# A two-layer perceiver on one core: another table of due times for the kernel's own planner

## The chip, the cores and the metric

The kernel runs on one core of one Trainium2 chip. The core has five engines with a queue of instructions each: PE (TensorE, matmuls and transposes, which write to PSUM), DVE (VectorE), ACT (ScalarE), POOL (GpSimd) and SP (SyncE, which here issues all DMA transfers). Each engine takes its own instructions strictly in the order in which the program has them, and waits on semaphores for what the others make. The metric is the time of one execution on the device in microseconds (us).

## The reference

128 sequences of 32 latent rows of 256 numbers (`x`) read a context of 257 rows each (`ctx_1024`). All is float32. Six steps, each added to `x`, each on a layer norm of `x`:

```python
x = x + _L0_xattn_ref(ctx_1024, ln(x), wq, wk, wv)   # softmax attention of x over the context
x = x + _L0_attn_ref(ln(x), W_in, W_gate, W_out, ...) # a selective scan along the 32 rows
x = x + _L0_ffn_ref(ln(x), W_fc, ln_w, ln_b, W_proj)  # gelu MLP with ternary weights
x = x + _L1_xattn_ref(ln(x), ctx, ctx, Wq, bq, ...)   # linear attention, focused feature map
x = x + _L1_attn_ref(ln(x), W_q, W_k, W_v, W_o, ...)  # attention over 32 rows, decaying scores
x = x + _L1_ffn_ref(ln(x), w1, b1, w2, b2)            # MLP with 8-bit activations, ternary weights
```

The scan is the recurrence `h = h * exp(A * d_t) + (x_t * d_t) * B`, `y_t = h @ c0`, over 512 channels with 16 states each.

## The kernel before

**Tiling.** Four sequences make a group of 128 rows, one tile of 128 partitions; there are 32 groups. The groups are taken in nine blocks, `BLOCKS = (2, 4, 4, 4, 4, 4, 4, 4, 2)`. In each block:

- `context_group` for each group: loads `x`, the context `cx` and its last row `cr`; transposes them on PE (`pT`, `pcT`); computes the query product `pq`, the scores `psc`, the softmax on ACT and DVE, `po`, `py`, and adds to `x`. A second part makes the keys and values that step four needs later: `pkey` (PE), `ku` (relu on ACT, then two products on POOL), `ks` (squares with sums on ACT), `kn` and `kf` (powers on POOL), `pval` (PE), `vf` (ACT) and `pk` (PE), whose result is `kvc`.
- `scan_block` for the whole block: gates and projections (`pproj` on PE), then, for each of four slices of channels and 16 states, `a` (exponential on ACT), `h` (the scan on DVE) and a weighted sum, `acc` on DVE or `h` and `some` on POOL. The last two blocks give six of the 16 states to POOL instead of two. It ends with `yg` on DVE and `pout` on PE.
- `latent_group` for each group: `mlp`, `linear`, `attention`, `quantized_mlp`, each a chain of short steps from engine to engine, and the store of the result.

Before the first block stands the setup of weights: among others the chain of small `sp_y` and `sp_z` operations on DVE, which leads to `isp`, `bkp`, `bk`, on PE `pisp`, `pbk`, `pkl`; loads of `w_in`, `w_gate`, `wv0` (in the profile `wv`) and others stand in SP's queue at the start.

**The planner.** The kernel doesn't issue its operations as the Python code meets them. A `Recorder` collects them all, with what each needs and an assumed duration (`ns_of`), and `Recorder.order` sorts them before anything is issued. A group of matmuls inside `R.together()` is one operation. `begin` and `part` cut the record into 251 spans: each `context_group` has two, each `scan_block` six, each `latent_group` four, the setup the rest. For each span the table `DUE` has a pair, the due time of its first operation and the end; operations between get due times in proportion to the assumed durations. One unit is about one block of the work. `AHEAD` is subtracted for transfers:

```python
a, b = self.spans[op.group]
due.append(a + (b - a) * (d - op.ns) / total[op.group] - AHEAD * ("sync" in op.ways))
```

The planner then places one operation after another. On each engine it looks at those that are ready, takes of those that could start within `WINDOW` ns of the earliest the one that is due first (`SOONER` favours those that free PSUM), and among the engines the one that would start first. `HORIZON` limits how far ahead of the oldest open work a buffer may be opened. An operation that two engines can do (a copy, a relu, the casts `x<-xT`) goes where its start plus its duration, weighed with `PRICE`, is least. The order of placing is the order in which all engines' queues are filled; a dependency without a semaphore keeps each engine's order. All of this runs when the program is built; on the chip only the resulting order is left.

**Lines in the profile.** Every recorded operation is issued by one line of `trace`, so nearly every row has the line L575 and is told apart by its tiles. L562 is `keep_busy`: where the plan leaves PE idle for more than `GAP` = 600 ns ahead of the first write to a bank of PSUM, it puts filler matmuls into that bank, `int(FILL * (op.gap - 200.0) / 216.0)` of them, with no result that anybody reads.

## Time and profile before

| | |
|---|---|
| three runs | 1745.08, 1747.30, 1744.87 us; median 1745.08 |
| the profiled execution | 1747.35 us, its span 1745.6 us |
| mean granted PE clock in it | 0.987 |
| matmuls of L562 | 172 |
| table loads on ACT | 95 shown, 121.9 us |
| DMA | 59.74 MB, mean 34 GB/s; 222 GB/s in the first 45 us |
| last `h` scan of the last block, end of its `yg` | 1633.1 us |
| last `yg` of the block before | 1509.3 us |

The costliest groups of instructions are the scans `h` on DVE (576 of them, 613.3 us), the exponentials `a` on ACT (576, 366.8 us), the sums `acc` on DVE (436, 299.5 us), and on PE `pval` and `pkey` (1024 each, 245.5 and 238.1 us). In a group's row the columns are engine and operation, out<-in by tile names, shapes, count, busy us and mean ns of one, and the idle time of that engine just before with what ended it. A mark in time such as "the last `yg` of a block" was found by putting the trace's instructions of each engine beside the recorded operations in order.

### The profile page before, as it was taken

The page shows a single profiled execution, that of the slowest core. Times are in us where ns is not written, and L with a number is a line of the kernel's source. Part 1 is how long each engine was busy: PE and PEld are TensorE (multiplying, and loading weights), DVE is VectorE, ACT ScalarE, POOL GpSimd, SP SyncE. Part 2 cuts the span into 40 slices and gives each one's busy share as a digit, 9 for nine tenths or more (in the row PEclk, how much of TensorE's full clock was granted, in tenths as well). Part 3 has the DMA queues.
Part 4 walks back from the last instruction along what each step waited for, and adds up shares of the span by engine and source line. Part 5 has one row for each costly group of instructions (what it writes and reads, how often), then busy time and mean ns, then how long its engine had stood idle before and what let it go on. Part 6 is the DMA issues. An engine that isn't in the chain of part 4 may idle for free.

```text
span 1745.6 us, 45752 instructions
## 1 busy us (share of the span) xinstructions
PE 1657.3 (95%) x17523; PEld 1203.7 (69%) x17591; DVE 1508.2 (86%) x2956; ACT 1426.8 (82%) x3495; POOL 1356.6 (78%) x2145
## 2 busy tenths in 40 slices
PE   8999999999999999999999999999999988888996
PEld 5777777776776777767777677776777665656663
DVE  5479689989988999988999799979999899988866
ACT  3677698889987999879887989888888898777665
POOL 4766758678776988778788779867888799878887
PEclk9999999999999999999999999999999999999998
DMA  7312000111000011001110021001110000000000
GB/s 221 107 45 86 29 29 29 45 41 32 10 29 29 8 64 38 29 2 41 35 35 29 8 62 41 29 2 35 41 35 29 4 23 1 7 1 2 8 8 19
DMA packets 44762, 59.74 MB, mean 34 GB/s; under 512 B 8704, under 2 KB 27008, under 8 KB 44544
## 3 DMA queue, kind: packets, MB, share of 16 engines
q1 hardware_dynamic: 44544, 56.81, 10.1%
q8 instruction: 139, 2.28, 0.6%
q14 instruction: 79, 0.65, 0.1%
HBM read 52.32 MB, written 4.19 MB: 32 GB/s over the span
## 4 chain that ended last, share of the span: by engine, by line
PE 39%; DVE 28%; ACT 14%; POOL 13%; issue 4%; DMA 0%; DVEq 0%; POOLq 0%; ACTq 0%
DVE h L575 13%; PE pval L575 6%; DVE acc L575 6%; PE pkey L575 6%; PE pproj L575 4%; ACT a L575 3%; PE pT L575 3%; POOL ku L575 2%; POOL rstd L575 2%; ACT ks L575 2%; PE pqa L575 2%; PE pmlp L575 2%; ACT L575 2%; PE pk L575 2%; DVE st L575 2%
## 5 line engine op out<-in xcount | busy, mean ns | idle before, releaser
L575 DVE TENSOR_TENSOR_SCAN h<-a,pproj 128x512 f32<-128x512 f32 (+1 forms) x576 | 613.3, 1086 | 22.4 <-ACT a L575 17.6
L575 ACT ACTIVATE a<-dl,a_neg 128x496 f32<-128x496 f32 (+1 forms) x576 | 366.8, 664 | 71.3 <-DVE h L575 68.4
L575 DVE SCALAR_TENSOR_TENSOR acc<-h,w_st,acc 128x512 f32<-128x512 f32 (+1 forms) x436 | 299.5, 687 | 0.6
L575 PE MATMUL pval<-wkv,cT 128*128 128x256 f32 x1024 | 245.5, 386 | 1.4 <-DVE y L575 1.3
L575 PE MATMUL pkey<-wkv,cT 128*128 128x256 f32 x1024 | 238.1, 386 | 0.0
L575 ACT ACTIVATE ks<-ku 128x256 f32<-128x256 f32 x512 | 209.0, 415 | 16.8 <-POOL ku L575 15.5
L575 PEld LDWEIGHTS pkey<-wkv,cT 128*128 128x128 f32 x1024 | 189.3, 190 | 38.0 <-issue 14.9
L575 PEld LDWEIGHTS pval<-wkv,cT 128*128 128x128 f32 x1024 | 188.9, 191 | 31.4 <-issue 2.8
L575 POOL TENSOR_TENSOR ku<-ku,e 128x512 f32<-128x512 f32 x128 | 162.7, 1281 | 33.9 <-ACT ku L575 28.3
L575 POOL TENSOR_TENSOR ku<-ks,ku 128x512 f32<-128x512 f32 x128 | 165.4, 1300 | 18.7 <-ACT ks L575 17.8
L575 POOL TENSOR_TENSOR kn<-kn,halves 128x4 f32<-128x4 f32 x128 | 131.1, 1026 | 24.4 <-ACT ks L575 23.4
L575 POOL TENSOR_TENSOR rstd<-rstd,halves 128x1 f32<-128x1 f32 x224 | 125.8, 565 | 7.3
L575 ACT ACTIVATE vf<-pval,kf 128x256 f32<-128x256 f32 x256 | 107.4, 472 | 23.2 <-PE pval L575 15.5
L575 ACT ACT_TABLE_LOAD x95 | 121.9, 1283 | 1.7
L575 PE MATMUL pproj<-xTs,w_in 128*128 128x512 f32 (+1 forms) x288 | 122.4, 552 | 0.3
L575 POOL TENSOR_SCALAR rstd<-mv 128x1 f32<-128x1 f32 x224 | 45.2, 202 | 96.6 <-DVE mv L575 73.2
L575 POOL TENSOR_TENSOR some<-some,h 128x512 f32<-128x512 f32 (+1 forms) x104 | 115.1, 1107 | 2.8
L575 PE MATMUL pmlp<-w_pr,hT 128*128 128x256 f32 x512 | 116.7, 381 | 0.0
L575 PEld LDWEIGHTS pmlp<-w_pr,hT 128*128 128x128 f32 x512 | 95.6, 190 | 13.8 <-issue 0.8
L575 ACT ACTIVATION_READ_ACCUMULATOR ks<-ku 128x1 f32 x512 | 100.6, 196 | 0.0
L575 POOL TENSOR_SCALAR h<-h,w_st 128x512 f32<-128x512 f32 (+1 forms) x104 | 65.3, 630 | 40.7 <-DVE h L575 35.5
L575 PE MATMUL ph<-w_fc,x 128*128 128x512 bf16 x350 | 89.2, 379 | 5.3 <-ACT ku L575 1.4
(291 smaller groups left out, 3883.7 us busy)
## 6 DMA issues: line engine op xcount, KB each, us to landing
cx<-in_ctx_dram SPq DMA_DIRECT2D x64, 512.0 KB
x<-in_x_dram SPq DMA_DIRECT2D x32, 128.0 KB
cr<-in_ctx_dram SPq DMA_DIRECT2D x128, 32.0 KB
out_dram<-x SPq DMA_DIRECT2D x32, 128.0 KB
vlz<-vl SPq DMA_DIRECT2D x128, 1.1 KB
w_in<-in_w_inT_dram SPq DMA_DIRECT2D x1, 1024.0 KB
raw_fc<-in_w_fcT_dram SPq DMA_DIRECT2D x2, 512.0 KB
raw_pr<-in_w_prT_dram SPq DMA_DIRECT2D x2, 512.0 KB
```

Source lines behind the costliest of these rows:

```text
L575: ins = getattr(engine, name)(*(traced(a) for a in args), **{k: traced(v) for k, v in kw.items()}).ins
```

## The change

Only numbers change: the five constants of the planner other than `GAP` and `FILL`, and nearly all of the 251 pairs of `DUE`. The operations that are recorded, their needs, their assumed durations and the code that places them are the same.

```diff
-PRICE = {"tensor": 0.0, "vector": 20.786091, "scalar": 1.959533, "gpsimd": 3.101899, "sync": 0.0}
-WINDOW = 13.816
-SOONER = 0.066
-AHEAD = 0.777235
-HORIZON = 1.581593
+PRICE = {"tensor": 0.0, "vector": 28.013093, "scalar": 4.356996, "gpsimd": 3.720234, "sync": 0.0}
+WINDOW = 13.821085
+SOONER = 0.0675
+AHEAD = 0.744939
+HORIZON = 1.665209
...
 DUE = (
-    (-1.0, -0.7651), (0.1, 0.598373), (-1.116179, -1.019716), (-0.267211, 0.164717),
-    (0.144, 0.184841), (0.213655, 0.218655), (0.394, 0.426463), (0.439863, 0.48282),
...
-    (8.366433, 8.49925), (8.732164, 8.864981), (8.847172, 8.866054), (8.489793, 8.799099),
-    (8.733373, 8.957995), (9.049952, 9.177105), (8.969544, 9.442262), (8.255137, 8.578091),
-    (8.559023, 8.723782), (8.443238, 8.947841), (8.98058, 9.391686),
+    (-1.233024, -0.335498), (0.019828, 0.480193), (-1.629912, -0.869437), (-0.837897, -0.738361),
+    (-0.093681, -0.088914), (-0.021839, -0.017211), (0.306149, 0.488484), (0.39917, 0.543159),
...
+    (8.253436, 8.258436), (8.822697, 8.893896), (7.808234, 8.023224), (7.738237, 8.019826),
+    (7.982233, 8.675198), (8.325431, 8.442062), (7.934126, 8.201542), (8.599655, 8.919463),
+    (8.003761, 8.776671), (8.022448, 8.742972), (9.092878, 9.902772),
 )
```

The fifth and sixth pairs are those of the first context group; the last eight those of the last two latent groups. A pair need not follow the one before it, and an operation is never due before those that it needs.

## The prediction

> **What bounds the kernel now.** I read the page's shares of busy time first, then the busy time by stretch, then the chain of waits, then the timeline of the first 30 us.

> ```profile
> span 1745.6 us, 45752 instructions
> PE 1657.3 (95%) x17523; PEld 1203.7 (69%) x17591; DVE 1508.2 (86%) x2956; ACT 1426.8 (82%) x3495; POOL 1356.6 (78%) x2145
> ...
> PE 39%; DVE 28%; ACT 14%; POOL 13%; issue 4%; DMA 0%; DVEq 0%; POOLq 0%; ACTq 0%
> ```

> PE looks full, but part of its busy time is filler (L562, matmuls that keep_busy puts where the plan sees PE idle). Counted on its own, with overlaps taken once, filler is 42 us, so PE does 1615 us of the program's matmuls, and 1745.6 - 1615.5 = 130 us hold none. The windows (columns: length, busy us of PE, PEld, DVE, ACT, POOL with counts, granted clock, DMA share, GB/s) tell where they are:

> ```profile
> 0.00:60.00 60.00, 54.28 (x279) 38.05 (x280) 28.39 (x82) 23.98 (x80) 33.27 (x68) 0.94 0.65 198
> 60.00:1360.00 1300.00, 1273.83 (x13700) 935.95 (x13749) 1153.28 (x2150) 1113.56 (x2801) 1007.49 (x1569) 1.00 0.11 34
> 1360.00:1509.30 149.30, 131.84 (x1181) 91.95 (x1188) 142.30 (x230) 126.43 (x268) 127.31 (x183) 1.00 0.03 9
> 1509.30:1633.10 123.80, 106.87 (x1152) 74.38 (x1156) 106.03 (x273) 89.90 (x208) 99.42 (x172) 0.94 0.01 4
> 1633.10:1745.60 112.50, 90.51 (x1216) 63.42 (x1221) 78.25 (x224) 72.89 (x140) 89.14 (x157) 0.92 0.04 12
> ```

> From 60 to 1360 us PE is 98% busy: it sets the pace, and an order can't gain there. To 1509.3 us (the end of the scans of the last block of four groups) DVE is at 95%. To 1633.1 us (the end of the very last scan) no engine is over 86%. Behind it, 112.5 us of short dependent steps with POOL highest at 79%. An order can gain in the last two stretches and in the first 60 us, nowhere else.

> **The change part by part.** No instruction is new. Counted in the two instruction streams: PE fillers 172 to 159, casts `x<-xT` on ACT 50 to 39 and on POOL 14 to 25, table loads 96 and 96, all else equal. So what is to be costed is the order. I weighed each step by the time the trace gave its kind and summed, engine by engine, what stands ahead of a mark.

> *Start.* The loads of x and cx of the first group now stand ahead of wv0, w_in and w_gate (1.8 MB), and on PE the first group's transposes, query product and scores (`pT`, `pq`, `pcT`, `psc`) stand ahead of `pbk` and `pkl`. Before, fillers stand there and PE waits:

> ```profile
> 11.79 2.32 PE L562 MATMUL pisp<-onesb,identb 128*128 128x512 bf16 x10
> 13.95 1.46 PE L562 MATMUL pbk<-onesb,identb 128*128 128x512 bf16 x6
> 16.16 0.71 PE L575 MATMUL pisp<-diag,ones 128*128 128x128 f32 x4 [0.76 <-DVE diag L575]
> ...
> 19.16 0.99 PE L575 MATMUL pbk<-ident,bkp 128*128 128x128 f32 x4 [2.07 <-DVE bkp L575]
> 20.67 0.37 PE L575 MATMUL pkl<-bk,onesb 3*128 3x256 bf16 x1 [0.52 <-DVE bk L575]
> ```

> Before, the first `pkey` starts at 27.85, after `pT`, `pq` and `pcT` from 22.83 to 26.89. With these done earlier and a `pT` of 0.4 us in their place it can start near 23.5: 4.35 us sooner. But behind it the new stream has 33 fillers where the old has 15 (58 and 57 in all at the start), since the next steps wait for POOL and ACT (`ku`, `ks`, `kn`), which follow `pkey` at their old speed: 18 holes more, which at 0.25 us, a `pisp` filler's own time (2.7 us for 11), take 4.5 us back. On DVE `st` and `mv` of the first x (0.42 and 0.18) now stand inside the sp_y chain, and `nmx` ahead of `bk`: should x land late, `diag`, `bkp` and so `pkl` are late by as much. Bounds -4.35 and 0.6 (the two operations); I take 0, since the holes only move.

> *60 to 1509.3 us.* Ahead of the mark stand 0.1 us more of PE, 1.4 more of DVE, 4.6 less of ACT, 7.2 more of POOL; seven lone fillers are gone, the 40 near its end stay 40. A filler's worth lies between those 0.25 us and all 130 us over 172, 0.76 us. So -1.8 to -5.3; I take -2, near the lower end, since the middle has few holes. What hides the 7.2 us of POOL is its share, 85% in the last 149 us; without that cover it costs 7.2 / 0.85 = 8.5 us.

> *To the last scan.* The stretch loses 7.0 us of DVE, 5.5 of PE, 4.6 of ACT, 9.6 of POOL, and its fillers go from 56 to 40. At the density it has now (106.2 us of DVE in 123.8, 86%) 7.0 us less is 8.2 us less. Bounds: -5.5 (PE's share alone) and -8.2 - 16 x 0.76 = -20 (the fillers' holes gone too). I take -8.

> *Behind the last scan.* What left the stretch is here: PE 81.1 to 86.4, DVE 73.7 to 79.3, ACT 70.8 to 76.6, POOL 90.1 to 96.5, fillers 12 to 21. Were the stretch to keep its density it would grow by 112.5 x 6.4 / 90.1 = 8.0 us; were the steps to fit into the idle 20% of POOL, by nothing. POOL and PE follow each other in the chain here, so I take +5.

> *Casts.* 0.405 us each on ACT, 0.397 on POOL: 11 moved are 4.4 us of work from one to the other, already in the sums. POOL can also hold DVE up:

> ```profile
> 1581.74 2.06 POOL L575 TENSOR_TENSOR kvx<-kvc,band 128x1088 f32<-128x1088 f32 x1
> 1582.02 2.06 DVE L575 TENSOR_TENSOR y<-y,zf 128x256 f32<-128x256 f32 x1
> ```

> That `y<-y,zf` takes 0.41 us elsewhere; here it ends with POOL's `kvx`. Eleven casts could cost DVE 0 to 4.4 us in this way; I take 0, as a cast is short and most sit where PE sets the pace. [...]

> The fillers also keep the clock up. Where PE waited at 17 to 19 us, the granted clock over 20 to 26 us was 0.50, and `pkl` took 674 ns a matmul against 386 for `pval`. [...]

> *Sum.* 0 - 2 - 8 + 5 + 0 = -5 us. A second way: 13 fillers fewer at 0.25 to 0.76 us are -3.3 to -9.9, and PE's own work is the same. The profiled execution took 1747.35 us (1.75 outside the span); with -5 that is 1742.35. The median of the runs is 1745.08, 2.27 below that execution, so the forecast for the median is 1740.

> **The rivals.**
> - *The end keeps its length.* The work that moved behind the last scan fits into gaps (PE has 22 us idle there, ACT 40). Then 0 - 2 - 8 + 0, and with 3 of the 4.35 us at the start -13: 1732. For it: no engine is over 79% there. Against: the last two groups run one step behind another from 1634 to 1743.
> - *All is given back.* The end grows by its full 8.0: -2, or 1743. For it: PE's work is the same, and every part that left one stretch stands in the next.
> - *GpSimd becomes the bound.* It has 7.2 us more ahead of 1509.3 and 6.4 more behind the last scan. At 85% and 80% that is +8.5 and +8.0, less 8.2 between: +8.3, or 1753, slower. It decides once POOL is over some 92% busy from 1360 to 1509 us. For it: the waits of DVE's `xn` for `rstd` and of PE for POOL's `q`, 12 us each. Against: its spare time there is 22 us.
> - *The plan isn't followed.* The order within an engine is fixed, but on the chip it waits for what is really late there, and the holes that the plan closed may open elsewhere: 1745, counted with "all is given back".

> **How the numbers follow.** Forecast (1740, itself 1735 to 1744) 0.36; end keeps its length (1732) 0.24; all given back or not followed (1743 to 1745) 0.17; GpSimd the bound (1753) 0.23. The range goes from 1727 (the -20 bound with +5, and a little of the start) to 1751, which leaves out the worst part of the last case and the best of the second. A measurement of this kernel tells 0.2%, 3.5 us. Faster than that is 1741.6 or less: all of the second case and nine tenths of the forecast's, 0.57; within, 0.20; slower, 0.23.

> **What would show it.** The last scan's end (1633.1 before) should come near 1623, and from there to the end should be 115 to 119 us; 112 or less speaks for the first rival, over 120 for the second. First `pkey` near 23.5 us, the start of the first pproj near its old 92 us. POOL from 1360 to 1509 under 90%. PE's filler rows 159. The forecast is wrong if the middle, 60 to 1360 us, moves by more than 3 us: I found nothing in it to move.

## The result and the profile after

The kernel after takes 1720.63 us (median of four runs, 1719.12 to 1721.22), the kernel before in the same session 1744.97 us (four runs, 1743.05 to 1747.30). The ratio is 0.9859, with a 95% interval of 0.9842 to 0.9876: faster by 24.3 us, where the prediction had 5, and below the low end of its range. The profiled execution of the kernel after took 1721.22 us, its span 1719.4.

First the lines of the page that answer to those shown of before (span, busy time by engine, chain of waits by engine):

```profile
span 1719.4 us, 45778 instructions
PE 1653.8 (96%) x17578; PEld 1203.7 (70%) x17578; DVE 1497.6 (87%) x2956; ACT 1422.8 (83%) x3484; POOL 1365.9 (79%) x2156
...
PE 50%; DVE 23%; ACT 14%; POOL 9%; issue 3%; DVEq 0%; POOLq 0%; ACTq 0%
```

PE's share of the chain that ended last rose from 39 to 50%, DVE's fell from 28 to 23 and POOL's from 13 to 9. Then the windows of the kernel after, cut at the same marks of the work (1493.3 us is the last `yg` of the last block of four groups, 1598.8 that of the last block, which ends the very last scan; the 1633.1 us of before is the same mark); columns as before:

```profile
0.00:60.00 60.00, 54.86 (x294) 39.09 (x295) 30.79 (x86) 25.27 (x83) 37.09 (x74) 1.00 0.65 198
60.00:200.00 140.00, 139.91 (x1567) 109.50 (x1567) 113.48 (x236) 109.14 (x336) 107.07 (x156) 1.00 0.22 67
200.00:1344.00 1144.00, 1130.10 (x12195) 824.35 (x12194) 1033.03 (x1914) 999.58 (x2451) 907.91 (x1422) 1.00 0.10 31
1344.00:1493.30 149.30, 133.50 (x1163) 92.25 (x1162) 141.07 (x230) 126.25 (x270) 128.09 (x186) 0.99 0.03 9
1493.30:1598.80 105.50, 96.17 (x943) 67.98 (x942) 97.18 (x249) 84.34 (x192) 90.23 (x154) 0.97 0.01 4
1598.80:1719.40 120.60, 99.31 (x1425) 70.57 (x1422) 82.05 (x243) 78.25 (x156) 95.51 (x169) 0.93 0.04 12
```

In the prediction's windows 60 to 1360 us of the kernel before was one row, with a clock of 1.00. Cut at 200 us it says more:

```profile
60.00:200.00 140.00, 135.30 (x1501) 106.54 (x1500) 112.12 (x233) 105.31 (x325) 91.00 (x138) 0.98 0.21 67
200.00:1360.00 1160.00, 1138.52 (x12201) 829.41 (x12250) 1041.16 (x1918) 1008.24 (x2477) 916.49 (x1432) 1.00 0.10 30
```

In the same 140 us the kernel before runs 1501 matmuls at a clock of 0.98 with 4.7 us idle, the kernel after 1567 at 1.00 with 0.1 us idle. The large differences are there and in the stretch before the last scan, which went from 123.8 to 105.5 us; the one behind it grew from 112.5 to 120.6.

The timeline of PE at the start of the kernel after, for the lines shown of before (start, length, engine, line, operation, tiles; in brackets the idle time before it and what ended it):

```profile
16.85 0.68 PE L575 MATMUL pisp<-diag,ones 128*128 128x128 f32 x4 [1.24 <-DVE diag L575]
17.37 0.60 PE L575 MATMUL pcT<-ident,cx 128*128 128x128 f32 x4
17.80 0.81 PE L562 MATMUL psc<-onesb,identb 128*128 128x512 bf16 x3
18.54 1.15 PE L575 MATMUL psc<-cT,qT 128*32 128x257 f32 x16
19.76 0.68 PE L575 MATMUL pbk<-ident,bkp 128*128 128x128 f32 x4
...
22.43 0.39 PE L575 MATMUL pkey<-bk,onesb 3*128 3x512 bf16 x2
```

`pbk` no longer waits 2.07 us; `pcT` and `psc` of the first group fill that place, and `pkey` starts at 22.43 (before: 27.85).

A ledger of PE's time shows where the 26.2 us of span went. Each interval of PE's rows is counted once, as the program's matmuls, fillers or idle; "lost by the clock" is an estimate, half the time of the program's matmuls that started while the granted clock was half (in before four `pkl` take 2.07 us at 20.97, where the clock is 0.50, and four `pval` of the same shape 1.03 us at 136.16, where it is 1.00). Where a filler overlaps the program's next matmul, the time goes to the one that started first, so that fillers come to 46.3 us here and to the prediction's 42 where they are counted only while they run alone.

| stretch (before; after) | length | idle | fillers | lost by the clock |
|---|---|---|---|---|
| to the end of the first block's scans (197.7; 188.2) | -9.5 | 10.4 to 5.1 | 14.8 to 14.9 | 6.2 to 0 |
| to the end of the sixth four-group block's scans (1355.6; 1339.4) | -6.7 | 21.4 to 14.0 | 1.9 to 0 | 0 to 0 |
| to the last `yg` of the seventh (1509.3; 1493.3) | +0.2 | 17.4 to 15.8 | 10.2 to 10.2 | 0 to 1.8 |
| to the end of the very last scan (1633.1; 1598.8) | -18.3 | 17.1 to 9.5 | 16.2 to 10.3 | 3.1 to 2.3 |
| to the end | +8.1 | 22.0 to 21.3 | 3.2 to 5.9 | 6.2 to 6.6 |
| sum | -26.2 | 88.3 to 65.7 | 46.3 to 41.3 | 15.5 to 10.7 |

Some idle time of before is missing records: without fillers its trace has 17,351 matmul records, that of after 17,419, and the program's matmuls at full clock come to 1595.6 and 1601.8 us. So about 6 us of the 22.6 less idle are not real, most of them in the second stretch, where 49 of the 68 missing records belong (the row from 200 to 1360 us has 12,201 matmuls for 12,250 weight loads). What is left is still more holes closed than the clock and the fillers together.

### The profile page after: what moved, and what is told of

Read it like the earlier page. It is cut to its first block, busy times and chain, and to the rows that moved or that the text cites. A ratio compares the mean times of both kernels' runs of the same rounds, so it can differ in the third digit from the quotient of the medians.

```text
span 1719.4 us, 45778 instructions
## 1 busy us (share of the span) xinstructions
PE 1653.8 (96%) x17578; PEld 1203.7 (70%) x17578; DVE 1497.6 (87%) x2956; ACT 1422.8 (83%) x3484; POOL 1365.9 (79%) x2156
## 4 chain that ended last, share of the span: by engine, by line
PE 50%; DVE 23%; ACT 14%; POOL 9%; issue 3%; DVEq 0%; POOLq 0%; ACTq 0%
DVE h L575 10%; PE pkey L575 8%; PE pproj L575 7%; PE pval L575 7%; DVE acc L575 5%; PE pT L575 3%; PE pmlp L575 3%; PE pqa L575 3%; ACT a L575 2%; PE pk L575 2%; POOL ku L575 2%; PE pka L575 2%; ACT L575 2%; PE pcT L575 2%; PE pq L575 2%
## 5 line engine op out<-in xcount | busy, mean ns | idle before, releaser
L575 DVE TENSOR_TENSOR_SCAN h<-a,pproj 128x512 f32<-128x512 f32 (+1 forms) x576 | 613.9, 1087 | 22.6 <-ACT a L575 12.2
L575 ACT ACTIVATE a<-dl,a_neg 128x496 f32<-128x496 f32 (+1 forms) x576 | 367.5, 664 | 57.8 <-DVE h L575 53.6
L575 DVE SCALAR_TENSOR_TENSOR acc<-h,w_st,acc 128x512 f32<-128x512 f32 (+1 forms) x436 | 299.9, 688 | 0.7
L575 PE MATMUL pval<-wkv,cT 128*128 128x256 f32 x1024 | 243.9, 384 | 0.1
L575 PE MATMUL pkey<-wkv,cT 128*128 128x256 f32 x1024 | 238.1, 386 | 0.0
L575 ACT ACTIVATE ks<-ku 128x256 f32<-128x256 f32 x512 | 209.1, 415 | 19.4 <-POOL ku L575 17.9
L575 PEld LDWEIGHTS pkey<-wkv,cT 128*128 128x128 f32 x1024 | 189.3, 190 | 39.0 <-issue 15.6
L575 PEld LDWEIGHTS pval<-wkv,cT 128*128 128x128 f32 x1024 | 188.0, 190 | 32.0 <-issue 4.5
L575 POOL TENSOR_TENSOR ku<-ku,e 128x512 f32<-128x512 f32 x128 | 163.0, 1282 | 31.2 <-ACT ku L575 29.9
L575 POOL TENSOR_TENSOR ku<-ks,ku 128x512 f32<-128x512 f32 x128 | 164.4, 1290 | 16.8 <-ACT ks L575 15.7
L575 POOL TENSOR_TENSOR kn<-kn,halves 128x4 f32<-128x4 f32 x128 | 134.6, 1055 | 23.4 <-ACT ks L575 21.8
L575 ACT ACTIVATE vf<-pval,kf 128x256 f32<-128x256 f32 x256 | 108.3, 475 | 31.1 <-PE pval L575 26.3
L575 POOL TENSOR_TENSOR rstd<-rstd,halves 128x1 f32<-128x1 f32 x224 | 126.1, 567 | 6.1
L575 PE MATMUL pproj<-xTs,w_in 128*128 128x512 f32 (+1 forms) x288 | 122.8, 554 | 2.2 <-DVE x L575 1.3
L575 POOL TENSOR_TENSOR some<-some,h 128x512 f32<-128x512 f32 (+1 forms) x104 | 115.2, 1108 | 3.5
L575 PE MATMUL pmlp<-w_pr,hT 128*128 128x256 f32 x512 | 117.3, 383 | 0.6 <-DVE x L575 0.6
L575 PEld LDWEIGHTS pmlp<-w_pr,hT 128*128 128x128 f32 x512 | 96.2, 191 | 14.7 <-DVE x L575 0.7
L575 POOL TENSOR_SCALAR h<-h,w_st 128x512 f32<-128x512 f32 (+1 forms) x104 | 65.4, 630 | 50.9 <-DVE h L575 32.6
L575 ACT ACTIVATION_READ_ACCUMULATOR ks<-ku 128x1 f32 x512 | 100.8, 197 | 0.0
L575 POOL TENSOR_SCALAR rstd<-mv 128x1 f32<-128x1 f32 x224 | 45.5, 203 | 67.5 <-DVE mv L575 43.3
L575 PE MATMUL ph<-w_fc,x 128*128 128x512 bf16 x384 | 91.5, 380 | 0.3 <-ACT vf L575 0.2
```

What stands on the lines that cost most here:

```text
L575: ins = getattr(engine, name)(*(traced(a) for a in args), **{k: traced(v) for k, v in kw.items()}).ins
```

## The experiments

Two kinds of edit were used. The first takes a part of the new table or the new constants alone. The second takes the planner out: the order is a fixed list of operations, each with its engine and its number of fillers, written down from the plans of the two kernels. With such a list the order of one stretch can be changed while the rest stays word for word. The two orders allow it, since at some places they have the same operations behind them but for a few: after 813 of the 9952 operations (154 us before) the two sets differ in 8 (four in each that the other lacks), after 2608 (476 us) in 14, after 7495 (1305 us) in 6.

### Parts of the table

Old and new pairs and constants were mixed: e1 has all new pairs with the old constants, e2 the reverse, e3 only the new pairs 0 to 30 (the first block and the contexts of the second), e4 only 203 to 250 (the last two blocks), both with the old constants. In e4, for example:

```diff
 DUE = (
...
-    (8.231279, 8.289197), (8.575174, 8.956992), (8.790837, 9.147175), (6.67874, 6.682632),
...
-    (8.559023, 8.723782), (8.443238, 8.947841), (8.98058, 9.391686),
+    (8.231279, 8.289197), (8.575174, 8.956992), (8.790837, 9.147175), (6.50929, 6.723457),
...
+    (8.003761, 8.776671), (8.022448, 8.742972), (9.092878, 9.902772),
```

> New table of due times, the five constants as before. The after kernel measured 1720.6 against 1745.0, a gain of 24.3 us; its marks moved by -9.5 us at the end of the first block's scans, by a further -6.6 up to the end of the last four-group block's scans, by a further -18.2 to the very last scan, and by +8.1 behind it. Theory A (the table carries it): 1718 to 1727, with the first block's scans ending near 188 us and the very last scan near 1600. Rival B (the constants carry it, since they set how the planner charges VectorE and ScalarE time): 1738 to 1748. Rival C (no part of the change carries it, any nudge of the plan moves the time by many us): anything, with marks that follow neither kernel.

> The old table with the new constants. Theory A (the table carries it): 1740 to 1750, the first block's scans ending near 197 us. Rival B (the constants): 1718 to 1727. Rival C (any nudge moves the time by many us): anywhere from 1730 to 1765, and then the three places of half clock (20 to 26, 132 and 173 us) may be gone or multiplied.

> Only the due times of pairs 0 to 30 are new (setup, contexts, scans and latents of the first block, contexts of the second), all else as before. Theory T1 (the first stretch gives 9.5 us by itself, 6.2 of it matmuls that no longer run at half clock, the rest waits, and it stays to the end since PE sets the pace behind it): 1734 to 1738, first block's scans ending at 188 to 189 us, no granted clock of half before 200 us. Rival (slack is given back: what starts sooner waits for VectorE at the end): the scans end near 188 but the time is 1742 to 1746. Rival C (any nudge moves all): the mark is near 188 and the time is far from both, below 1730 or above 1750.

> Only the due times of pairs 203 to 250 are new (the contexts, scans and latents of the last four-group block and the last block). Theory T3 (the stretch to the very last scan loses 18 us, the work behind it takes 8 more): 1733 to 1737, the very last scan ending some 15 to 18 us sooner than in the kernel before, near 1616, and 118 to 122 us behind it. Rival (the last part fits only with an earlier middle, so the new due times are out of step with it): 1743 to 1755, last scan near 1630. The marks before 1300 us should be as before, within 2 us; where they are not, a change of due times of the end reaches back through the planner.

| kernel | median us | ratio to before (95%) | end of first block's scans | last `yg` of the seventh four-group block | very last scan |
|---|---|---|---|---|---|
| before | 1747.55 | | 197.7 | 1509.3 | 1633.1 |
| e1, new pairs | 1794.81 | 1.0273 (1.0254 to 1.0292) | 191.5 | 1550.4 | 1672.4 |
| e2, new constants | 1788.78 | 1.0238 (1.0217 to 1.0259) | 195.9 | 1553.3 | 1678.5 |
| e3, first pairs | 1773.47 | 1.0151 (1.0132 to 1.0171) | 189.2 | 1531.0 | 1667.7 |
| e4, last pairs | 1788.91 | 1.0236 (1.0218 to 1.0253) | 198.4 | 1535.9 | 1671.7 |

All four are slower, by 26 to 47 us; theories A, B, T1 and T3 all missed, and so did the rivals of e3 and e4 that had the time near that of before (1742 to 1755). Rival C, that any nudge of the plan moves the time by many us, is nearest: e1 and e3 are as it said, e2 lies even beyond its 1730 to 1765. Neither the pairs nor the constants carry the gain by themselves. e3 shows how: its first block's scans end at 189.2 us with no half clock before 200, as T1 had it, but at the scans' ends of the blocks behind it is 6.9 us ahead (third block), 1.1 ahead (fifth), then 11.8 late (seventh) and 21.7 late (eighth). e4 is within 0.7 us of before up to 1156 us, 4.2 late at the seventh block and 26.6 at the eighth. The windows of e4:

```profile
0.00:1156.00 1156.00, 1131.40 (x11952) 830.80 (x11953) 1001.64 (x1884) 965.82 (x2462) 877.23 (x1379) 0.99 0.14 44
1360.00:1500.00 140.00, 116.13 (x855) 69.78 (x853) 106.44 (x176) 87.75 (x174) 89.75 (x130) 0.94 0.03 9
```

and the second of these stretches in the kernel before:

```profile
1360.00:1500.00 140.00, 122.88 (x1137) 84.31 (x1143) 133.00 (x211) 122.60 (x257) 121.62 (x175) 1.00 0.03 10
```

In the same 140 us e4 has 855 matmul rows for 1137, DVE at 106 us for 133, ACT at 88 for 123: work of several groups that used to overlap isn't ready at the same time. A pair says when a piece of work is due relative to all others, so a part of the table in the old surroundings is a new plan, and a worse one. These runs say nothing of what each stretch of the good order is worth.

### Stretches of the order

The list in place of the planner:

```diff
-        for i in self.order():
-            op = self.ops[i]
+        for i, e, n in PLACED:
+            op, self.ops[i].engine = self.ops[i], ENGINES[e]
...
-            if op.engine == "tensor" and op.gap > GAP:
-                self.keep_busy(op)
+            if n:
+                self.keep_busy(op, n)
```

`PLACED` is one kernel's list up to a cut and, behind it, what is left in the order of the other's list.

> No table decides here: each engine's order is a fixed list, the after kernel's for the first 2608 of the 9952 operations (up to 476 us in the before kernel), the before kernel's for all behind. Where both traces had the same 2608 operations done, the after kernel stood 10.3 us ahead. Theory D (the gain is a sum of local gains, and PE, which sets the pace, hands each on to the end): 1733 to 1737, that is 8 to 12 us less than before. Rival E (what starts sooner is given back behind, where VectorE sets the pace to 1509 us): 1742 to 1746. Rival F (orders only work as a whole): 1750 or more, as the four kernels with half of the table gave.

> The before kernel's order for the first 2608 operations and behind operation 7495 (1305 us), the after kernel's between them. Between these two marks the after kernel won 17.4 - 10.3 = 7.1 us (4.1 of them from 1134 us on). Theory D (local gains that add): 1736 to 1740. Rival of the prediction (an order can't gain where PE is 98% busy; the 7 us are something that the earlier start brought): 1743 to 1747. Rival F (orders only work as a whole): 1750 or more.

> The before kernel's order up to operation 7495 (1305 us), the after kernel's for the rest: the last third of the scans of the sixth four-group block, the last block of four and the last block of two. From this mark on the after kernel won 27.1 - 17.4 = 9.7 us. Theory D (local gains that add): 1733 to 1738, with the last scan some 17 us sooner than before (near 1616) and 118 to 122 us behind it. Rival E (the last stretch gained only because all stood earlier): 1742 to 1746. Rival F: 1750 or more. If D holds in all three, the three gains add up to 24 to 27 us.

> The after kernel's order for the first 7495 operations (1305 us in the before kernel), the before kernel's behind. Alone, the start gave 8.2 us and the middle 1.3; the after kernel stood 17.4 us ahead at this mark. Theory D (gains simply add): 1734 to 1737. Rival J (the middle's order was made for a start that comes sooner, and gives its 7 us only behind it): 1726 to 1731, with the frontier some 17 us ahead at operation 7495. Rival K (the rest is in the profiled runs' scatter): between them.

> The before kernel's order for the first 813 operations (154 us) and behind operation 7495 (1305 us), the after kernel's between. At operation 813 the after kernel stood 7.7 us ahead, at 7495 it stood 17.4 ahead: 9.7 by the marks. The middle cut at operation 2608 gave only 1.3 where the marks said 7.1. If the cut itself ate it (behind it that run lost some 3 us against the after kernel within 60 us, while the order changed over, and had one spell of half clock twice as long): 1734 to 1738. If the middle's order needs the earlier start wherever it is cut (some 6 us short again): 1740 to 1744.

> The after kernel's order for the first 813 operations only (154 us), the before kernel's behind. By the marks 7.7 us: 1736 to 1739, and no half clock at 19 and 132 us, but the one at 173 us stays. If it is the waits of the loads and of the setup that count, not these 154 us as a whole, less remains: 1740 to 1743. Added to the run with the other cut it should give the 15.5 us that start and middle gave together, if the cuts cost nothing.

The last columns tell how far each profiled run stood ahead (minus) of the profiled run of before, at the end of PE's last instruction among the first 813, 2608, 7495 and all operations. That run of before took 1747.35 us, some 2 more than the medians, so the marks at the end say some 2 us too much; the medians decide:

| operations in after's order | median us | before | ratio (95%) | at 154 | at 476 | at 1305 | end |
|---|---|---|---|---|---|---|---|
| all (after) | 1720.63 | 1744.97 | 0.9859 (0.9842 to 0.9876) | -7.7 | -10.3 | -17.4 | -26.1 |
| e5, 0 to 2608 | 1737.29 | 1745.44 | 0.9956 (0.9943 to 0.9968) | -7.2 | -9.8 | -10.0 | -11.0 |
| e6, 2608 to 7495 | 1744.10 | 1745.44 | 0.9994 (0.9985 to 1.0003) | -0.4 | 1.1 | -2.3 | -3.7 |
| e7, 7495 to the end | 1736.85 | 1745.44 | 0.9951 (0.9939 to 0.9964) | 0.1 | 0.1 | -0.5 | -8.9 |
| e9, 0 to 7495 | 1729.82 | 1745.33 | 0.9912 (0.9899 to 0.9926) | -8.0 | -10.5 | -17.7 | -16.7 |
| e13, 813 to 7495 | 1736.43 | 1745.11 | 0.9960 (0.9948 to 0.9973) | -2.3 | -3.0 | -8.9 | -8.5 |
| e14, 0 to 813 | 1738.11 | 1745.11 | 0.9966 (0.9952 to 0.9980) | -7.8 | -8.7 | -8.7 | -9.2 |

Theory D, that what a stretch wins stays won, holds in the main. In e5 the 10 us of the start are still there 800 us later (its median is 0.3 us above D's range). e14, e13 and e7 together cover the whole program, and their gains, 7.0, 8.7 and 8.6 us, each known to some 2 us, add up to 24.3, the gain of the whole change.

Two runs spoke against it at first. e6 gave 1.3 us for the 7.1 of the marks, within the range of the prediction's own rival (an order can't gain there), and e9 came out at 1729.82, not in D's range but in J's: the middle gives its gain only behind an earlier start. e13, with the middle cut at 154 us and the old start, gave 8.7 for the 9.7 of after's marks, and e14 and e13 together (15.7) give what e9 gave (15.5). So the order behind 154 us doesn't need the earlier start. What e6 lacks lies at its cut and in the mark there: the kernel after stood 12.3 us ahead at operation 2560 and 10.3 at 2608, so that the 7.1 were rather 5.1, and e6, 13.4 us behind after at operation 2560, was 15.1 behind at 2660, with the change-over between them, and 15.1 at 7495. The last 2 us are the profiled run of before: against it e6 stands 3.7 ahead at the end, but that run is 1.9 above the median of before in e6's session.

Two marks were not as expected. e14 has no half clock at 173 us either: behind the new start the wait ahead of `pmean` of `w_pr` is gone. And e13 stands 2.3 us ahead at 154 us with before's own order to there; its profile has 3.4 us of half clock to there where that of before has 10.2, which the last section takes up.

### Fillers in the order of before

The order of before, with 26 fillers more, at the three waits ahead of half clock (an entry is operation, engine, fillers):

```diff
-    [91, 0, 6], ... [1037, 0, 0], ... [389, 0, 0]
+    [91, 0, 14], ... [1037, 0, 8], ... [389, 0, 10]
```

> The before kernel's order throughout, with 26 more filler matmuls: 8 ahead of pbk (PE waited there 2.07 us for bkp at 17 us), 8 ahead of the pT of o at 129 us (2.17 us), 10 ahead of pmean of w_pr at 171 us (2.53 us). Behind each of these waits the records show PE at half clock, for 6.8, 3.4 and 3.4 us. Theory G (of the 12.8 us won in the first 257 us, about 6 are the clock that these waits cost): no half clock before 200 us, the first block's scans end 5 to 7 us sooner (191 to 193), time 1738 to 1741. Rival H (the half clock costs nothing since other engines set the pace there, the waits themselves are what counts): mark and time within 1.5 us of before, 1743.5 to 1746.5. Rival I (the clock does not follow the waits): half clock stays at these places, and the time grows by up to 2 us.

1741.87 us against 1745.44, ratio 0.9980 (0.9972 to 0.9989): 3.6 us. That is nearest to G, whose range it misses by 0.9 us; H and I are out. No half clock is left before 1423 us, and the first block's scans end at 192.4. The timeline of PE in the kernel before, at two of the waits:

```profile
128.31 1.13 PE L575 MATMUL pproj<-xTs,w_in 128*128 128x256 f32 x4
131.61 0.44 PE L575 MATMUL pT<-ident,o 128*128 128x128 f32 x2 [2.17 <-DVE o L575]
131.88 3.48 PE L575 MATMUL pval<-wkv,cT 128*128 128x256 f32 x8
...
169.77 1.04 PE L575 MATMUL pcT<-ident,cx 128*128 128x128 f32 x8
173.34 4.98 PE L575 MATMUL pmean<-w_pr,ones 128*128 128x256 f32 x15 [2.53 <-DVE w_pr L575]
```

and at the first of them in e8:

```profile
127.56 1.89 PE L562 MATMUL pT<-onesb,identb 128*128 128x512 bf16 x8 [0.21 <-DVE gm L575]
129.51 0.44 PE L575 MATMUL pT<-ident,o 128*128 128x128 f32 x2
129.79 1.89 PE L575 MATMUL pval<-wkv,cT 128*128 128x256 f32 x8
```

Eight `pval` take 3.48 us behind the wait and 1.89 behind the fillers: 1.6 us that the wait costs in this profile on top of itself. The windows of e8 have the clock at 1.00 in both stretches where before has 0.94 and 0.98:

```profile
0.00:60.00 60.00, 55.98 (x297) 38.69 (x298) 29.56 (x86) 24.99 (x84) 35.16 (x71) 1.00 0.65 198
60.00:200.00 140.00, 139.45 (x1564) 108.62 (x1563) 113.39 (x232) 107.25 (x332) 94.25 (x141) 1.00 0.22 67
```

By 257 us e8's profile is 5.3 us ahead of that of before, the kernel after's 10 to 13, depending on the operation. So some 5 are what the clock gave between these two profiles (3.6 by the medians), and the rest is order: the waits are gone too.

### The last block's slices held back

The order of after, with the operations of the last block's four scan slices at the places that the list of before gives them, and all operations still behind what they need:

> The after kernel's order, but the scan slices of the last block stand where the before kernel has them: the last slice's first pproj goes from place 8825 of the 9952 back to 9045 (before: 9051), its last sum ends at place 9287. Theory L (the earlier last slice carries the 8.6 us of the end): the last scan ends 12 to 20 us later than in the after kernel (1611 to 1619), and the time is 1726 to 1731. Rival M (it is the rest of the end that carries it, the work behind the last scan is laid differently): the last scan ends later as well, but the stretch behind it gets shorter by as much, and the time is 1719 to 1723.

1748.02 us, ratio 1.0020 (1.0011 to 1.0029): 27.4 us more than after, far beyond L's 6 to 10; M is out. The run stood 19.2 us ahead of before at operation 8562, like the kernel after (19.7). Then the last scan ended at 1628.4 us instead of 1598.8. One window of e10:

```profile
1500.00:1560.00 60.00, 44.74 (x351) 30.91 (x351) 50.81 (x122) 43.92 (x97) 45.04 (x79) 0.91 0.01 3
```

and the same of the kernel after:

```profile
1500.00:1560.00 60.00, 55.78 (x467) 38.59 (x466) 53.56 (x136) 49.25 (x113) 52.19 (x89) 0.97 0.01 4
```

PE does 116 matmuls less in these 60 us, with 15 us idle instead of 4 and a lower clock. In the kernel after the first `pproj` of the last slice comes at 1529.4 us, amid the latents of the block before; in the kernel before at 1587.4, behind slice three. So the rest of the new end doesn't carry the gain without the early slice. The 27.4 us aren't the slice's worth in the kernel before, since the held order suits neither plan and, like e1 to e4, may lose for that alone; what the whole new end is worth is in e7, 8.6 us, with the last scan 15.9 earlier and 7 given back behind it.

### The casts

The order of after; of the 25 casts `x<-xT` whose engine the new plan changed, 18 go back from POOL to ACT and 7 from ACT to POOL.

> The after kernel's order, with the 25 casts that the new plan gave to another engine back on the engine of the before kernel (18 from POOL to ACT, 7 from ACT to POOL). The prediction took 0 for them. If so: 1718.5 to 1722.5. Rival N (POOL holds DVE up, the prediction's upper bound of 4.4 us): 1715 to 1718. Rival O (the plan put them where ACT was late, so that moving them was part of the gain): 1724 to 1730.

1719.61 us, ratio 0.9855 (0.9842 to 0.9868), against 0.9859 for the kernel after: no difference. N and O are out. As the only other change is the list in place of the planner, the list itself costs nothing that these runs can tell.

### Fillers in the order of after

> The after kernel's order with 60 more fillers at eleven places behind 1440 us, ahead of matmuls for which PE waited over 0.9 us there (pqT, poq, pT, poa, pya), each wait filled but for some 0.3 us. From 1440 us on the after kernel did 21.3 us of matmuls at half clock. Theory G (as at the start of the before kernel, where 26 fillers took away three spells of half clock and gave 3.6 us): half clock behind 1440 us goes from 33 us to under 15, time 1712 to 1717. Rival P (there the steps wait for other engines, so a faster PE only waits longer): the half clock goes, the time stays, 1718.5 to 1722. Rival Q (a filler ahead of a chain's next step makes it late where the wait is shorter than planned): 1722 to 1728.

Of the 60 fillers 22 were really issued: `keep_busy` leaves out tiles that aren't float32, and `pqT` is bf16. 1717.09 us, ratio 0.9840 (0.9826 to 0.9853), 3.5 below the kernel after, though the two intervals overlap; e11, in the same session as e12, took 2.5 more, and their runs don't overlap. The time is at the upper edge of G, the clock isn't: within the span half clock behind 1440 us went from 27.3 us (the expectation said 33) to 21.4, not to under 15. Nothing was changed ahead of the `pqT`, so the next run gives 36 of the missing 38 fillers in the bank of the `poq` that follows:

```diff
-        for i, e, n in PLACED:
+        for i, e, n, at in PLACED:
...
-                self.keep_busy(op, n)
+                self.keep_busy(self.ops[at], n)
```

> The after kernel's order with the 22 fillers that the last run with fillers really had (keep_busy leaves out tiles of bf16, so those meant for the places ahead of pqT were not issued: 181 filler matmuls in it, 159 in the after kernel), and 36 more, put ahead of four pqT into the bank of the poq behind, where PE waited 3.37, 1.41, 2.14 and 2.51 us between 1685 and 1707 us. If the clock counts there: no half clock from 1680 to 1705 us, and 1713 to 1716. If the chain through POOL's q sets the pace there: half clock gone, time as before, 1716.5 to 1718.5. If the bank of poq is not free in time and the fillers hold pqT up: 1719 or more.

1715.28 us (four runs, 1714.38 to 1717.25), ratio 0.9836 (0.9823 to 0.9850), and no half clock from 1440 to 1706 us: the first outcome. The timeline of PE in the kernel after, at the longest of these waits:

```profile
1684.67 0.59 PE L575 MATMUL phq<-w,qT 128*128 128x512 bf16 x2
1688.64 0.62 PE L575 MATMUL pqT<-identb,q 128*128 128x128 bf16 x8 [3.37 <-POOL q L575]
1689.10 2.58 PE L562 MATMUL poq<-onesb,identb 128*128 128x512 bf16 x6
```

and in e15:

```profile
1677.87 0.59 PE L575 MATMUL phq<-w,qT 128*128 128x512 bf16 x2
1678.30 2.97 PE L562 MATMUL poq<-onesb,identb 128*128 128x512 bf16 x13
1681.83 0.62 PE L575 MATMUL pqT<-identb,q 128*128 128x128 bf16 x8 [0.56 <-POOL q L575]
1682.29 2.32 PE L562 MATMUL poq<-onesb,identb 128*128 128x512 bf16 x10
```

`pqT` still starts when POOL's `q` is there, 3.97 and 3.96 us after the start of the last `phq`. What is won lies behind: ten fillers take 2.32 us where six took 2.58. Half clock over the whole span is down to 3.6 us from 27.3. e15 is the fastest kernel of this study: 5.3 us below the kernel after, and its highest run, 1717.25, is below the lowest of the kernel after, 1719.12. But the two were timed in different sessions, and their intervals against before overlap a little (up to 0.9850 and from 0.9842). Its step from e12, 1.8 us, is within the two intervals.

## Why the prediction was wrong

The sign was right, and so were some steps; the sum was a fifth of what came.

- **"From 60 to 1360 us PE is 98% busy: it sets the pace, and an order can't gain there."** This is the step that failed. PE does set the pace, and just for that reason each wait it loses shows in the time. e13 gives 8.7 us for the order from 154 to 1305 us (which of its moves give them wasn't tested), and most of e14's 7.0 lies behind 60 as well: at operation 631 (121 us) the kernel after was only 2.0 ahead, at 813 it was 7.7. The row said 98%, and 2% of 1300 us are 26 us (some 4 of them rows that the trace lacks), several times the forecast; I called that nothing. And busy isn't full speed: the clock read 1.00 as a mean over 1300 us, while two spells of half clock, 3.41 us each, sat at 132.02 and 172.98 us. The bound of -5.3 for this term came from fillers, which stand only where the plan saw a hole of over 600 ns; the holes that closed (`pT` of `o`, 2.17 us; `pmean` of `w_pr`, 2.53) had none.
- **Start, 0 us.** By itself nearly right: 2.0 us at 121 us, within its bounds, and the first `pkey` at 22.4 for 23.5. The argument that the 18 more fillers only move the holes held for the time in fillers (14.8 and 14.9 us to 60 us) but left out the clock.
- **The clock.** The waits of 2.07, 2.17 and 2.53 us ahead of 200 us cost PE 6.2 us of speed in the profile of before, by the ledger, and e8 gave 3.6 us of time, by the medians, for filling them. The prediction read the half clock behind the first of them (0.50 over 20 to 26 us), put nothing for it into the sum, and looked for no other such wait.
- **To the last scan, -8 us.** -18.3 by the marks: inside the bounds of -5.5 and -20, near the far end. 7.6 of it are idle time and 5.9 fillers. Where I kept the density of the stretch, the order raised it: PE's idle time and fillers fell from 33.3 of 123.8 us to 19.8 of 105.5.
- **Behind the last scan, +5 us.** +8.1, its upper bound. The rival "all is given back" had this part right (8.0), and was wrong in that the part before it is larger.
- **Casts, 0 us.** Right within what the runs can tell: in e11 putting the casts back changed the time by 1.0 us, within the intervals, and nothing of the bound of 4.4 us is seen.
- **GpSimd as the bound.** POOL came to 128.09 of 149.3 us, 86%, below the 92 from which it was to decide. That rival fell by its own sign. So did "the plan isn't followed": e13, e14 and e7 show the gain of each stretch on the chip.
- **The signs.** Filler rows 159 and POOL under 90%: right; first `pkey` 22.4 for 23.5 and first `pproj` 89.5 for 92: near. The last scan's end, 1598.8 for 1623, and the middle, which was to stay within 3 us and gained some 15 (2.0 ahead at 121 us, 17.4 at 1305), told that the forecast was wrong. The 120.6 us behind the last scan were the sign of the second rival, which the time refutes.

## What to carry to other kernels

Where an engine sets the pace at 98%, look at the remaining 2% one wait at a time: here the few us that an order closed there stayed won to the end. Read the granted clock in short windows, not as a mean, and in more than one run, since behind the same wait of some 2.2 us on TensorE the kernel before had 3.4 us at half clock and e13 none. To learn what a planner's change does, put its result in as a fixed order and exchange stretches where both orders have the same work behind them; exchanging parts of its inputs makes other plans, and here worse ones.

## What the runs showed of the hardware that was not expected

- A wait of PE of 2.17 us with PE busy on both sides was followed by 3.4 us at half clock (132 us in the kernel before); with all but 0.21 us of it filled (e8) there was none. One such pair of profiles proves little: e6, e7 and e13 have before's order up to that wait and wait 2.15 to 2.16 us there; in e6 and e7 half clock follows, in e13 it doesn't. The timeline of PE in e13:

```profile
131.02 0.44 PE L575 MATMUL pT<-ident,o 128*128 128x128 f32 x2 [2.16 <-DVE o L575]
131.29 1.89 PE L575 MATMUL pval<-wkv,cT 128*128 128x256 f32 x8
```
